# Cross-attention of a decoder layer: VectorE's instructions in written order, with the softmax cut into parts

## The chip, the cores and the metric

The kernel runs on one core of one Trainium2 chip. The metric is the device time in microseconds (us) of one execution; the number used for comparing is the median of several. A core has five engines that run side by side and wait for each other by semaphores: TensorE (PE in the profile, with its weight loads as PEld), VectorE (DVE), ScalarE (ACT), GpSimd (POOL) and SyncE (SP), which here issues most of the DMAs.

## The reference

One decoder layer on 32 sequences of 64 tokens (2048 rows) of width 512, all float32. Self-attention, cross-attention and a feed-forward block follow each other, each with a residual and a layer norm. The change touches only the cross-attention:

```python
q = (query @ Wq + bq).reshape(B, L, NKV, G, HDIM)      # 8 groups of G = 4 heads of 128
k_, v_ = jnp.split(kv @ Wkv + bkv, 2, axis=-1)
scores = jnp.einsum('blkgd,bmkd->bkglm', q, k) * scale # 64 x 64 for each sequence and head
attn = jax.nn.softmax(scores, axis=-1)
o = jnp.einsum('bkglm,bmkd->blkgd', attn, v).reshape(B, L, NHEAD * HDIM)
return o @ Wo + bo
```

Then `x = layernorm(x + that)`.

## The kernel before

**Stages.** Self-attention comes first, then the keys and values of the cross-attention (`keys_values`), then the cross-attention itself with the feed-forward block woven into its end. In the trace the cross-attention's first product starts at 2054.78 us.

**Units.** The cross-attention runs over 32 units, g (group of four heads, outer) by tb (block of 512 tokens, inner); N is 32. Iteration n of the main loop computes the queries and scores of unit n, and the attention output and output projection of unit n-1. So each iteration holds two big products: the queries of unit n (tiles `qx`, L282) and the projection of unit n-1 (tiles `wx`, L282).

**Seven products for eight.** Each big product is made of seven half-size products (Strassen's scheme in Winograd's form), called steps 1 to 7. A step is four matmuls in the code and eight in the trace, and fills one of three PSUM banks, x, y or z: steps 1 and 2 use x, steps 6, 7 and 4 use y, steps 5 and 3 use z. A later step of a bank adds onto what is in it, so it may start only when VectorE has read the bank as it stood before. For the projection these reads are additions into `acc` (L345, and L353 for the second read of step 1). The code's order of the steps is 1, scores, 6, 5, 2, 7, 3, 4 for the projection, and 1, 6, 5, 7, 2, 4, attention output, 3 for the queries. The next use of a bank thus sets a due time for a read: the read of step 7 (bank y) is due at step 4, with step 3 alone between them on PE; the read of step 6 is due at step 7, that of step 5 at step 3, that of step 1 at step 2. For the queries the read of step 6 (L322) is due at step 7, with step 5 between.

**The softmax of a unit** comes in two halves by tokens, pr = 0 and 1. For each: the largest score (L1056, VectorE), the difference (L1058, VectorE), the exponential (L1059, ScalarE), the sum (L1061), its reciprocal (L1062), the product with it (L1063) and a transpose in 32 x 32 blocks into tile T (L1068), the last four on VectorE. Then `move` issues eight DMAs from SP that put T into pT (L1082), which the next iteration's attention output (`attend`, PE L1103) reads.

**Who sets the order.** The loop runs under a manual schedule for PE and POOL: these two keep the order as written. VectorE, ScalarE and SP are ordered by a scheduler with its own costs, which moves their instructions among each other where dependencies allow. So VectorE's order in the program is not the code's: the scheduler puts the read of step 2 and the read of step 7 behind most of the softmax.

**The layer norm of a block** runs after the last group's projection of it (g = 7, iterations 29 to 32). `layernorm` at L1136 issues statistics (L149, L150), a sum (L151), a square root (ACT, L152), a reciprocal (L155) and four scalings (L157); the block's transposes (PE L129) are put off into the next iteration behind step 2 of its queries.

**POOL** makes sums of tokens (L1206 to L1211, `next_tokens`), of attention outputs (L256 to L259), of weights (L190 to L199) and, for g = 0, adds a bias to `acc` (L1261); all read and write SBUF.

Of the kernel before, what the change touches and what calls it, by code (L numbers as in the profile page):

```python
# [21 lines left out]
SEQ = 64  # L22
TB = 512
NTB = NT // TB
# [7 lines left out]
SQ = 32  # L32
# [20 lines left out]
def decoder_layer(  # L53
# [30 lines left out]
    nc = tc.nc  # L84
# [3 lines left out]
    small = ctx.enter_context(tc.tile_pool(name="small", bufs=4))  # L88
# [48 lines left out]
    def layernorm(tb, name):  # L137
        for part in layernorm_parts(tb, name):
            part()
# [324 lines left out]
    with ExitStack() as ph:  # L464
# [4 lines left out]
        sb = ph.enter_context(tc.tile_pool(name="sa", bufs=2))  # L469
# [168 lines left out]
        def turn(n, i):  # L638


            nc.vector.transpose(  # L641
                Ts[n][:, :, i, :], ps_.pop((n, i)).rearrange("q (b k) -> q b k", k=SQ)
            )

        def move(n, ranges=range(NQD), queue=nc.sync):


            if n // 2 not in pTs:
                pTs[n // 2] = sb.tile([P, NQD, NPC, P], F32, tag="pT", name=f"pT{n // 2}")
# [46 lines left out]
        N = len(units)  # L696
# [121 lines left out]
        for n in range(N):  # L818
            b, h = divmod(n, REP)
            g, r = units[n][0], n % PER  # L820
# [117 lines left out]
    with ExitStack() as ph:  # L938
# [14 lines left out]
        def load_xq(g):  # L953
            src = xwq[:, g * REP * HD : (g + 1) * REP * HD]
            wq_cur[g] = load_left(src, f"xwq{g}", nc.gpsimd)
# [91 lines left out]
                            )  # L1047
                ss[n, pr] = s

        def softmax(n, pr):  # L1050
            g, tb = units[n]
            u = f"x{g}_{tb}_{pr}"
            s = ss.pop((n, pr))
            shape = [P, 2 * REP, SEQ]
            mx = small.tile([P, 2 * REP], F32, tag="mx", name=f"mx{u}")
            nc.vector.tensor_reduce(mx, s, AX.X, ALU.max)  # L1056
            e = sb.tile(shape, F32, tag="e", name=f"e{u}")
            nc.vector.tensor_tensor(e, s, mx[:, :, None].to_broadcast(shape), ALU.subtract)  # L1058
            nc.scalar.activation(e, e, AF.Exp, scale=SCALE)  # L1059
            den = small.tile([P, 2 * REP], F32, tag="xden", name=f"den{u}")  # L1060
            nc.vector.tensor_reduce(den, e, AX.X, ALU.add)  # L1061
            nc.vector.reciprocal(den, den)  # L1062
            nc.vector.tensor_tensor(e, e, den[:, :, None].to_broadcast(shape), ALU.mult)  # L1063


            if pr == 0:
                Ts[n] = sb.tile([P, 2, TPB * REP, SQ], F32, tag="T", name=f"Tx{g}_{tb}", bufs=1)
            nc.vector.transpose(  # L1068
                Ts[n][:, :, pr * 2 * REP : (pr + 1) * 2 * REP, :].rearrange("p k r j -> p r k j"),
                e.rearrange("p r (k i) -> p r k i", i=SQ),  # L1070
            )

        def move(n):
# [54 lines left out]
        def project(n, *steps):  # L1128
            g, tb = units[n]
            for i in steps:  # L1130
                pjs[n].step(i)
                pjs[n].read()
            if steps[-1] == 4:
                del pjs[n]
                if g == NKV - 1:
                    layernorm(tb, "x")  # L1136
                    later.append(lambda: transpose_block(tb, "x2"))


# [74 lines left out]
        N = len(units)  # L1214
        load_kv(0)

        ph.enter_context(tc.manual_schedule(
            engines={mybir.EngineType.PE, mybir.EngineType.Pool}
        ))


        for n in range(N + 1):
            if n < N:
                g, tb = units[n]
                q = queries(n)
                for i in (1, 6, 5, 7):
                    q.step(i)
                    q.read()
                q.corner()
                q.step(2)  # L1230


                behind = g > 0 and tb == 1
                if not behind:
                    next_tokens(n + 1, 0)
            while later:
                later.pop(0)()
            if n < N:
                q.step(4)
                q.read()  # L1240
            if n > 0:
                attend(n - 1)
            if n < N:
                q.step(3)
                q.read()
                if behind:
                    next_tokens(n + 1, 0)
                next_tokens(n + 1, 1)
            if n == N:
                feed_forward(1)  # L1250
            if n > 0:
                project(n - 1, 1)
            if n < N:
                if n + 1 < N:
                    load_kv(n + 1)
                scores(n)
                softmax(n, 0)
            if n < N and g == 0:
                for j in range(TPB):
                    a = acc[tb][:, j, :]  # L1260
                    nc.gpsimd.tensor_tensor(a, a, bo, ALU.add)  # L1261
            if n > 0:
                project(n - 1, 6, 5)
            if n < N:
                softmax(n, 1)
                move(n)
                if tb == NTB - 1 and g + 1 < NKV:
                    load_xq(g + 1)
            if n > 0:
                project(n - 1, 2, 7, 3, 4)  # L1270
                if n < N and tb == 0:
                    if g > 0:
                        load_xo(g)
                    if g == NKV - 1:
                        load_ffn()
            if n == N - 1:
                feed_forward(0)
        feed_forward(2)
        while later:
            later.pop(0)()  # L1280
# [50 lines left out]
```

## Time and profile before

| what | us |
|---|---|
| median of 3 runs | 3100.44 (3098.5 to 3103.58) |
| the profiled execution: its own time | 3099.28 |
| the profiled execution: span from first to last instruction | 3097.0 |
| PE busy over the span | 3038.2 (98%) |
| VectorE busy | 2184.0 (71%) |
| POOL busy | 967.6 (31%) |
| ScalarE busy | 754.8 (24%) |
| self-attention, keys and values (0 to 2054.78) | 2054.78 |
| iterations 0 to 28 of the cross-attention, to the attention output of iteration 29 (2054.78 to 2894.10) | 839.32 |
| the last group's iterations with layer norms (2894.10 to 2977.80) | 83.70 |
| the feed-forward end (2977.80 to 3097.0) | 119.20 |

The granted TensorE clock is 0.998 over the span. In the stage from 2054.78 to 2894.10 PE is busy for 827.80 us of 839.32, VectorE for 515.24. Busy shares are averages: a matmul's end is modelled, and what an iteration could save is read from the places where PE stands still, and from the length of an iteration that has no such place. In the profile "issue" means that an engine waited for nothing that is shown, and "idle <- X" names what released it.

### The profile page before, as it was taken

The numbers are of one execution on the slowest core, as the hardware profiler recorded it, in microseconds if no ns is written. First come the engines' busy times: TensorE is split into PE (matmuls) and PEld (weight loads), VectorE is DVE, ScalarE is ACT, GpSimd is POOL, SyncE is SP. The second block draws the span as 40 slices with busy tenths as digits, with TensorE's granted clock in tenths as the row PEclk, the third lists the DMA queues.
The fourth block names the chain that finished last, engine by engine and source line by source line (L and its number), as shares of the span: only waits on it lengthen the run. The fifth ranks groups of instructions, "written<-read, shape, count | busy, mean of one in ns | idle before, by whom it ended". The sixth has DMA issues, their size and how long they took to land.

```text
span 3097.0 us, 42303 instructions
## 1 busy us (share of the span) xinstructions
PE 3038.2 (98%) x14944; PEld 2318.1 (75%) x14944; DVE 2184.0 (71%) x3957; ACT 754.8 (24%) x1760; POOL 967.6 (31%) x789
## 2 busy tenths in 40 slices
PE   8999999999999999999999999999999999999998
PEld 6777677777777777777677769988888888888864
DVE  6777777877877877877877754346656656656777
ACT  2323222222222232232322321211111111111132
POOL 4231321321322322323222122135444444444421
PEclk9999999999999999999999999999999999999999
DMA  6444444444444444444344343321121121121101
GB/s 206 116 114 119 113 115 123 111 122 114 108 128 112 106 128 113 107 125 118 101 123 109 98 126 128 109 103 48 50 67 48 51 66 48 51 66 48 49 28 41
DMA packets 200913, 298.66 MB, mean 96 GB/s; under 512 B 44160, under 2 KB 94848, under 8 KB 200704
## 3 DMA queue, kind: packets, MB, share of 16 engines
q1 hardware_dynamic: 187328, 282.51, 33.7%
q10 hardware_dynamic: 11328, 9.26, 1.0%
q0 software_dynamic: 2048, 4.20, 0.5%
q8 instruction: 120, 1.97, 0.3%
q14 instruction: 89, 0.73, 0.1%
HBM read 107.05 MB, written 20.97 MB: 41 GB/s over the span
## 4 chain that ended last, share of the span: by engine, by line
PE 86%; DVE 10%; DMA 1%; SPq 1%; issue 1%; ACT 1%; DVEq 0%; ACTq 0%
PE po L661 15%; PE s L615 15%; PE pox L1103 2%; DVE acc L345 2%; SPq L653 1%; PE w_0y L282 1%; PE q_3y L282 1%; PE w_3y L282 1%; PE qx_3y L282 1%; PE qx_2y L282 1%; PE qx_0y L282 1%; PE q_2y L282 1%; PE w_1y L282 1%; PE qx_1y L282 1%; PE wx_3y L282 1%; PE q_0y L282 1%
## 5 line engine op out<-in xcount | busy, mean ns | idle before, releaser
L623 ACT ACTIVATE p<-s,nmax 128x576 f32<-128x576 f32 x512 | 379.2, 741 | 1211.6 <-DVE nmax L620 1173.1
L615 PE MATMUL s<-kT,qT 128*128 128x288 f32 x2048 | 578.0, 408 | 11.5 <-ACT p L623 10.7
L661 PE MATMUL po<-pT,v 128*128 128x512 f32 (+1 forms) x1280 | 549.1, 602 | 4.3 <-DMA pT<-T 4.3
L615 PEld LDWEIGHTS s<-kT,qT 128*128 128x128 f32 x2048 | 387.4, 190 | 116.4 <-issue 20.1
L620 DVE TENSOR_REDUCE nmax<-s 128x1 f32<-128x576 f32 x512 | 384.0, 750 | 47.5 <-PE s L615 45.3
L641 DVE STREAM_TRANSPOSE T<-p 128x576 f32<-128x576 f32 x512 | 394.0, 769 | 4.4
L661 PEld LDWEIGHTS po<-pT,v 128*128 128x128 f32 (+1 forms) x1280 | 213.7, 189 | 204.2 <-issue 176.9
L633 DVE TENSOR_SCALAR p<-p,den 128x576 f32<-128x576 f32 x512 | 325.5, 636 | 17.9
L632 DVE RECIPROCAL den<-den 128x1 f32<-128x1 f32 x512 | 83.9, 164 | 238.2 <-ACT p L623 220.0
L256 POOL TENSOR_TENSOR so<-oT,oT 128x512 f32<-128x512 f32 x32 | 42.6, 1330 | 651.0 <-ACT oT L684 651.0
L258 POOL TENSOR_TENSOR so<-oT 128x512 f32<-128x512 f32 x32 | 40.7, 1272 | 334.4 <-PE w_1y L282 93.0
L1209 POOL TENSOR_TENSOR txx<-x1T 128x512 f32<-128x512 f32 x31 | 39.3, 1267 | 244.4 <-PE qx_3z L282 94.1
L197 POOL TENSOR_TENSOR tx<-xT 128x512 f32<-128x512 f32 x31 | 39.7, 1280 | 206.9 <-PE q_3z L282 65.5
L623 ACT ACTIVATION_READ_ACCUMULATOR p<-s,nmax 128x1 f32 x512 | 99.0, 193 | 0.0
L1059 ACT ACTIVATE ex<-ex 128x512 f32<-128x512 f32 x64 | 39.3, 630 | 203.1 <-DVE ex L1058 203.1
L256 POOL TENSOR_TENSOR sox<-oTx,oTx 128x512 f32<-128x512 f32 x32 | 40.5, 1266 | 149.7 <-DVE oTx L1123 144.3
L684 ACT COPY oT<-po 128x512 f32<-128x512 f32 x128 | 71.8, 586 | 44.9 <-PE po L661 44.1
L1043 PEld LDWEIGHTS sx<-kvx,qTx 128*64 128x64 f32 x2048 | 62.3, 138 | 10.6 <-issue 10.6
L1121 ACT ACTIVATE oTx<-pox,bv 128x256 f32<-128x256 f32 x128 | 52.0, 470 | 66.4 <-PE pox L1103 66.4
L1043 PE MATMUL sx<-kvx,qTx 128*64 128x64 f32 x2048 | 66.7, 224 | 0.0
L1103 PE MATMUL pox<-pTx,kvx 64*128 64x256 f32 x512 | 64.5, 389 | 0.1
L1123 DVE TENSOR_SCALAR oTx<-pox,bv 128x256 f32<-128x256 f32 x128 | 53.6, 478 | 9.8 <-PE pox L1103 9.8
(445 smaller groups left out, 5779.9 us busy)
## 6 DMA issues: line engine op xcount, KB each, us to landing
pT<-T SPq DMA_DIRECT2D x1020, 80.0 KB
pT<-T SPq DMA_DIRECT2D x1016, 64.0 KB
xT<-in_xT SPq DMA_DIRECT2D x31, 1024.0 KB
kvx<-kv SPq DMA_DIRECT2D x32, 512.0 KB
pTx<-Tx SPq DMA_DIRECT2D x256, 64.0 KB
kv<-c SPq DMA_DIRECT2D x30, 512.0 KB
wo<-in_woT SPq DMA_DIRECT2D x32, 256.0 KB
xwq<-in_xwq SPq DMA_DIRECT2D x32, 256.0 KB
```

The lines of the kernel that those rows point to most:

```text
L256: nc.gpsimd.tensor_tensor(t[1], a[1, 0], a[1, 1], ALU.add)
L282: nc.tensor.matmul(self.banks[b][:, m, :], self.left[i][:, k, m * P : (m + 1) * P], self.right[i][:, k, :], start=(first and m + k == 0), ...
L615: nc.tensor.matmul(s[:, a, :HALF], qTs[n // REP][:, units[n][2], i * P : (i + 1) * P], kTs[g][:, a * HALF : (a + 1) * HALF], start=True, s ...
L620: nc.vector.tensor_reduce(nmax, s[:, :, :HALF], AX.XY, ALU.max, negate=True)
L623: nc.scalar.activation(p.rearrange("q (a k) -> q a k", a=2), s[:, :, :HALF], AF.Exp, bias=nmax, accum_out=den,)
L632: nc.vector.reciprocal(den, den)
L633: nc.vector.tensor_scalar(p, p, den, None, ALU.mult)
L641: nc.vector.transpose(Ts[n][:, :, i, :], ps_.pop((n, i)).rearrange("q (b k) -> q b k", k=SQ))
L661: nc.tensor.matmul(pos[n].rearrange("d (a q) -> d a q", a=NQD), vs[units[n][0]][rows, v, :], pTs[n // 2][rows, :, chunk, :], skip_group_ch ...
L684: nc.scalar.copy(o[:, i, :].rearrange("d (t a k) -> d a t k", t=TPB, a=NQD), pos.pop(n - 1 + i).rearrange("d (a t k) -> d a t k", a=NQD, t ...
L1043: nc.tensor.matmul(s[b * SEQ : (b + 1) * SEQ, i * REP + h, :], qTs[n][:, h, pr * HF + c0 : pr * HF + c0 + SEQ], kvs[n][:, pr, 0, c0 : c0 + ...
L1103: nc.tensor.matmul(po[pr, b][:, i, :].rearrange("d (h a j) -> d h a j", h=REP, a=2), kvs[n][r, pr, 1, i * HD : (i + 1) * HD], pTs[n][r, :, ...
```

## The change

VectorE joins the engines under the manual schedule for iterations 0 to 30; at iteration 31 that schedule is closed and one for PE and POOL alone is opened, as before. `softmax` is cut into five parts (`largest`, `exponentials`, `denominators`, `weights`, `turn`), and these are called for both halves between the steps of the projection, in this order: step 1, scores; largest 0 and 1; exponentials 0 and 1; step 6; denominators 0 and 1; step 5; weights 0; steps 2 and 7; weights 1; step 3; turn 0 and 1; `move`; step 4. A `Projection` step's read is issued right after its product. `load_xq` of the next group is written ahead of steps 2 and 7. The layer norm of a block is split: statistics and square root directly after step 4, the reciprocal and scalings from a list `scales`, which is emptied after the first query step of the next iteration that has one, and ahead of the transposes.

In the built program the order of instructions on PE, ScalarE and POOL stays as it was. On SP, in the seven iterations that load the next group's output weights, the fourth of these loads (`xwo_3`) now stands ahead of the eight DMAs of `move` and not behind them. On VectorE the instructions are the same in number and kind, in another order.

```diff
-        def softmax(n, pr):
+        def largest(n, pr):
+            mxs[pr] = small.tile([P, 2 * REP], F32, tag="mx", name=f"mx{n}_{pr}")
+            nc.vector.tensor_reduce(mxs[pr], ss[n, pr], AX.X, ALU.max)
+        def exponentials(n, pr):
...
+            nc.vector.tensor_tensor(e, s, mxs[pr][:, :, None].to_broadcast(shape), ALU.subtract)
             nc.scalar.activation(e, e, AF.Exp, scale=SCALE)
+        def denominators(n, pr):
+            nc.vector.tensor_reduce(den, es[pr], AX.X, ALU.add)
+        def weights(n, pr):
             nc.vector.reciprocal(den, den)
+            nc.vector.tensor_tensor(
+                e, e, den[:, :, None].to_broadcast([P, 2 * REP, SEQ]), ALU.mult
+            )
+        def turn(n, pr):
...
             nc.vector.transpose(
...
-                    layernorm(tb, "x")
+                    stats, scale = layernorm_parts(tb, "x")
+                    stats()
+                    scales.append(scale)
                     later.append(lambda: transpose_block(tb, "x2"))
...
-        ph.enter_context(tc.manual_schedule(
-            engines={mybir.EngineType.PE, mybir.EngineType.Pool}
-        ))
+        units_order.enter_context(tc.manual_schedule(engines={
+            mybir.EngineType.PE, mybir.EngineType.Pool, mybir.EngineType.DVE
+        }))
...
         for n in range(N + 1):
+            if n == N - 1:
+                units_order.close()
+                ph.enter_context(tc.manual_schedule(
+                    engines={mybir.EngineType.PE, mybir.EngineType.Pool}
+                ))
...
                 for i in (1, 6, 5, 7):
                     q.step(i)
                     q.read()
+                    while scales:
+                        scales.pop(0)()
...
                 scores(n)
-                softmax(n, 0)
+            parts(n, (largest, 0), (largest, 1), (exponentials, 0), (exponentials, 1))
...
+            steps(n - 1, 6)
+            parts(n, (denominators, 0), (denominators, 1))
+            steps(n - 1, 5)
+            parts(n, (weights, 0))
+            if n < N and tb == NTB - 1 and g + 1 < NKV:
+                load_xq(g + 1)
+            steps(n - 1, 2, 7)
+            parts(n, (weights, 1))
+            steps(n - 1, 3)
+            parts(n, (turn, 0), (turn, 1))
+            if n < N:
+                move(n)
             if n > 0:
-                project(n - 1, 6, 5)
-            if n < N:
-                softmax(n, 1)
-                move(n)
-                if tb == NTB - 1 and g + 1 < NKV:
-                    load_xq(g + 1)
-            if n > 0:
-                project(n - 1, 2, 7, 3, 4)
+                steps(n - 1, 4)
```

More of the change, by code (lines that the diff above doesn't have):

```diff
@@ L1048, in scores @@
                 ss[n, pr] = s
-        def softmax(n, pr):
+        def largest(n, pr):
+            mxs[pr] = small.tile([P, 2 * REP], F32, tag="mx", name=f"mx{n}_{pr}")
+            nc.vector.tensor_reduce(mxs[pr], ss[n, pr], AX.X, ALU.max)
+        def exponentials(n, pr):
             g, tb = units[n]
-            u = f"x{g}_{tb}_{pr}"
             s = ss.pop((n, pr))
             shape = [P, 2 * REP, SEQ]
[L1055 to L1058, printed above, removed]
+            es[pr] = e = sb.tile(shape, F32, tag="e", name=f"ex{g}_{tb}_{pr}")
+            nc.vector.tensor_tensor(e, s, mxs[pr][:, :, None].to_broadcast(shape), ALU.subtract)
             nc.scalar.activation(e, e, AF.Exp, scale=SCALE)
-            den = small.tile([P, 2 * REP], F32, tag="xden", name=f"den{u}")
-            nc.vector.tensor_reduce(den, e, AX.X, ALU.add)
-            nc.vector.reciprocal(den, den)
-            nc.vector.tensor_tensor(e, e, den[:, :, None].to_broadcast(shape), ALU.mult)
+        def denominators(n, pr):
+            dens[pr] = den = small.tile([P, 2 * REP], F32, tag="xden", name=f"denx{n}_{pr}")
+            nc.vector.tensor_reduce(den, es[pr], AX.X, ALU.add)
+        def weights(n, pr):
+            e, den = es[pr], dens[pr]
+            nc.vector.reciprocal(den, den)
+            nc.vector.tensor_tensor(
+                e, e, den[:, :, None].to_broadcast([P, 2 * REP, SEQ]), ALU.mult
+            )
+        def turn(n, pr):
+            g, tb = units[n]
             if pr == 0:
@@ L1069, in softmax @@
                 Ts[n][:, :, pr * 2 * REP : (pr + 1) * 2 * REP, :].rearrange("p k r j -> p r k j"),
-                e.rearrange("p r (k i) -> p r k i", i=SQ),
+                es[pr].rearrange("p r (k i) -> p r k i", i=SQ),
             )
@@ L1215, in decoder_layer, with parts, steps @@
         load_kv(0)
-        ph.enter_context(tc.manual_schedule(
-            engines={mybir.EngineType.PE, mybir.EngineType.Pool}
-        ))
-        for n in range(N + 1):
+        units_order = ExitStack()
+        units_order.enter_context(tc.manual_schedule(engines={
+            mybir.EngineType.PE, mybir.EngineType.Pool, mybir.EngineType.DVE
+        }))
+        def parts(n, *made):
+            for part, pr in made:
+                if n < N:
+                    part(n, pr)
+        def steps(n, *made):
+            if n >= 0:
+                project(n, *made)
+        mxs, es, dens, scales = {}, {}, {}, []
+        for n in range(N + 1):
+            if n == N - 1:
[3 more added lines that the diff above has]
+                ))
             if n < N:
@@ L1235, in decoder_layer @@
                     next_tokens(n + 1, 0)
+            while scales:
+                scales.pop(0)()
             while later:
@@ L1250, in decoder_layer @@
                 feed_forward(1)
-            if n > 0:
-                project(n - 1, 1)
+            steps(n - 1, 1)
             if n < N:
@@ L1261, in decoder_layer @@
                     nc.gpsimd.tensor_tensor(a, a, bo, ALU.add)
-            if n > 0:
-                project(n - 1, 6, 5)
-            if n < N:
-                softmax(n, 1)
-                move(n)
-                if tb == NTB - 1 and g + 1 < NKV:
-                    load_xq(g + 1)
-            if n > 0:
-                project(n - 1, 2, 7, 3, 4)
+            steps(n - 1, 6)
[8 more added lines that the diff above has]
+            parts(n, (turn, 0), (turn, 1))
+            if n < N:
+                move(n)
+            if n > 0:
+                steps(n - 1, 4)
                 if n < N and tb == 0:
@@ L1277, in decoder_layer @@
                 feed_forward(0)
+        scales.pop(0)()
         feed_forward(2)
```

## The prediction, made before the changed kernel ran

> **What bounds the kernel now.** I read the busy table first (PE 98%), then what PE waits for in the cross-attention, from the first attention output to the feed-forward (2081 to 2978 us). Columns: us in total, times, longest.
>
> ```profile
> PE wx_2y L282 <- DVE acc L345: 6.8, 8, 0.9
> PE wx_0y L282 <- DVE acc L345: 3.8, 8, 0.6
> PE wx_1y L282 <- DVE acc L345: 1.3, 2, 0.7
> PE x L129 <- ACT qTx L317: 1.0, 2, 0.5
> PE x L129 <- DVE x1T L131: 0.6, 2, 0.3
> ```
>
> PE stands still 18 times for a projection read on VectorE, 11.9 us in all. The weight load runs ahead of the matmuls and has to be refilled after a stop, so the loss is larger. The table of stages, cut at the starts of two successive attention outputs (L1103), gives it (columns: stage, length, busy time of PE, PEld, DVE, ACT, POOL, clock, DMA share, GB/s):
>
> ```profile
> 2256.18:2285.87 29.69, 28.77 (x194) 24.44 (x194) 18.64 (x32) 4.27 (x9) 15.37 (x12) 1.00 0.18 49
> 2285.87:2314.38 28.51, 28.51 (x194) 24.52 (x194) 17.43 (x32) 4.27 (x9) 9.86 (x8) 1.00 0.28 75
> ```
>
> The second has no stop and takes 28.51, all of it PE; the first has one stop of 0.92 and is 1.18 longer. So a stop costs 0.26 to 0.27 beyond its idle time, and 28.51 is PE's floor for an iteration. The 28 stretches from 2081.20 to 2894.10 take 812.90; at the floor 28 x 28.51 = 798.28. Excess 14.6. Why VectorE is late shows in the timeline of a stalled iteration (start, length, idle before):
>
> ```profile
> 2384.11 1.26 POOL L192 TENSOR_TENSOR xwq<-xwq,xwq 128x512 f32<-128x512 f32 x1
> 2384.31 1.61 DVE L1063 TENSOR_TENSOR ex<-ex,denx 128x512 f32<-128x512 f32 x1
> ...
> 2387.53 0.68 DVE L345 TENSOR_TENSOR acc<-wx_2x,acc 128x512 f32<-128x512 f32 x1
> 2388.13 0.70 DVE L1068 STREAM_TRANSPOSE Tx<-ex 128x512 f32<-128x512 f32 x1
> 2388.75 0.65 DVE L345 TENSOR_TENSOR acc<-wx_2y,acc 128x512 f32<-128x512 f32 x1
> 2388.85 4.95 SPq L1082 DMA_DIRECT2D pTx<-Tx  x8
> 2389.33 0.67 DVE L345 TENSOR_TENSOR acc<-wx_2z,acc 128x512 f32<-128x512 f32 x1
> 2389.45 1.59 PEld L282 LDWEIGHTS wx_2y<-xwo,oTx 128*128 128x128 f32 x8 [1.32 <-DVE acc L345]
> 2389.45 1.99 PE L282 MATMUL wx_2y<-xwo,oTx 128*128 128x256 f32 x8 [0.92 <-DVE acc L345]
> ```
>
> The read of step 7 stands behind both products and both transposes of the softmax. A product (L1063) that meets a POOL instruction takes 1.61 instead of 0.65; its median over all 64 is 0.68, its longest 1.63. That tips the scheduler's order over: step 7's read comes at 2388.75, after PE has finished step 3. Iterations in which POOL is quiet have the same order and no stop.
>
> **Part 1: the new order, step by step.** I count from the start of step 6 on PE (2379.64 in the iteration shown), with 1.73 for a product and 0.60 from one VectorE instruction to the next. A read can start 0.20 after its product's nominal end. Unchanged up to the differences: step 6's read at 2.22. Sums 2.8 to 4.0. Step 5's read 4.0 to 4.6. Reciprocal, then product 0 from 4.8 to 5.4 (6.3 if blocked as shown). Step 2's read is ready at 5.4, so done by 6.0 (6.9 if blocked). Step 7's read is ready at 7.1 and done at 7.75, while PE wants it at 8.6, after step 3. Margin 0.85 in quiet and busy iterations. Product 1 from 7.9 to 8.5, step 3's read 8.8 to 9.4, the transposes to 10.7, step 4's read to 11.3. The other due times: step 6's read 2.8 against 5.2, step 5's 4.6 against 6.9, and step 4's 11.3 against 13.8 (its bank comes round to the third query product). So the 18 stops go. What is late next on PE? Nothing but itself, in these stretches.
>
> Of the 14.6 above, 0.37 of the first stretch are no stop (its first attention output took 2.28, not 1.93): 14.2. Iterations 29, 30 and 31 lie behind 2894.10 and have a stop each, idle 0.46, 0.61 and 0.61, so about 0.7, 0.9 and 0.9: 2.5. Iteration 31 is ordered by the scheduler again; in the built program step 7's read there stands behind one product and one transpose only, which fits. Gain of part 1: 16.7.
>
> **The rule weighed.** Product 0 still stands ahead of step 7's read. [...] Blocked by two (2 x 1.27), product 0 ends at 8.0 and step 7's read at 9.2: 0.6 late, 0.9 with the refill, in the same 18 iterations, and part 1 gains nothing. The row speaks for one: none of 64 exceeded 1.63. I take the row.
>
> **Part 2: what else moves.** `move`: the transposes end at 10.7 instead of 9.2 (7.9 when quiet), so its eight DMAs start 1.5 to 2.9 later; issuing them takes 4.95. The attention output that needs them starts at 21.0. In iteration 0 the first was issued at 2075.09 and the attention output ran at 2081.13 without waiting, so they land in 6.0 or less: by 16.9. Cover 4.1; without it each us costs 31 us over the kernel. SP: `xwo_3` now goes ahead of them in seven iterations; it waits for step 3, done at 8.6, and one such issue takes 0.37, so it is gone before 10.8. It lands earlier than before, which only helps POOL's sums (L196). `load_xq` keeps its place on SP. New semaphore waits: VectorE now waits for PE at each read with product 1, the transposes and so on queued behind; all these have the margins above. Zero.
>
> **Part 3: iteration 0.** Nothing is projected, so the new order only changes the halves' interleaving: product 0 now waits for its reciprocal directly (about 0.2), and difference 0 waits behind largest 1, whose scores end at 2069.05. I get the transposes' end 0.35 later. There PE already waited 1.3 for the query read behind them (qx_1y for L322). Loss 0.35 (bounds 0 and 0.8).
>
> **Part 4: iteration 30, the layer norm.** Statistics and scalings of block 0 are now ordered by the code, ahead of the read of the query's step 6 (L322), which step 7 of the queries needs. Before:
>
> ```profile
> 2915.28 0.17 DVE L151 TENSOR_SCALAR rstd_x<-mv_x 128x4 f32<-128x4 f32 x1
> ...
> 2916.53 0.69 DVE L322 TENSOR_TENSOR qTx<-qx_2y,qTx 128x512 f32<-128x512 f32 x1 [1.08 <-PE qx_2y L282]
> 2916.63 0.21 ACT L152 ACTIVATE rstd_x<-rstd_x 128x4 f32<-128x4 f32 x1
> 2917.14 0.17 DVE L155 RECIPROCAL rstd_x<-rstd_x 128x4 f32<-128x4 f32 x1
> 2917.35 3.85 DVE L157 TENSOR_SCALAR acc<-acc,mv_x,rstd_x 128x512 f32<-128x512 f32 x4
> 2917.78 1.70 PEld L282 LDWEIGHTS qx_2y<-txx,xwq 128*128 128x128 f32 x8
> 2917.99 1.89 PE L282 MATMUL qx_2y<-txx,xwq 128*128 128x256 f32 x8
> ```
>
> The read slipped in ahead of the scalings. Now count from the first query product: step 4's read ends at 1.0; four blocks' statistics at 0.84 each (0.72 to the aggregate, 0.12 more) bring L151 to 4.4; the square root to 4.8 (its table load fits behind the first query copy); reciprocal 5.1; scalings from 5.3. Alone four of them take 1.92 (as at 2949.77), against POOL's token sums 3.85 as here: to 7.25 or 9.15. These sums are there again, from 5.4. L322 ends at 7.9 or 9.8; PE wanted it at 5.2. Loss 2.7 or 4.6 idle, 3.0 or 4.9 with the refill. I take 4.8, since two of POOL's three sums fall there (the third waits for step 7 itself). Iteration 31's query read is put ahead by the scheduler again (done at 4.8 against 5.2), and the transposes follow as before: zero, at most 1.
>
> **Sum.** 16.7 - 0.35 - 4.8 = 11.5. The profiled execution took 3099.28 (span 3097.0 and 2.3 around it): 3087.8. The median of the runs is 1.16 higher: 3100.44 - 11.5 = 3088.9.
>
> **Rivals.**
> - *Iteration 30 costs less*: scalings that miss POOL, or start earlier: 1 to 3. Gain 13.5 to 16: 3084.5 to 3087. For it: the bound 3.0. Against: POOL's sums are released by PE at the same moment. 0.10.
> - *Half of the stops stay or move*: product 0 or 1 meets POOL twice, or a read in written order misses its slot in some iterations. Gain 2 to 9: 3091.5 to 3098.5, about 3095. Against: margin 0.85 and the longest row 1.63. 0.13.
> - *The DMAs of `move` come late* (slower): they decide once the time from first issue to landing passes 10.2. At 11.2, 31 attention outputs wait 1.0: 31 - 11.5, so 3120. For it: `move` is the one thing that got later in every iteration. Against: 6.0 seen, DMA share 0.14 to 0.28 there. 0.03.
> - *It doesn't do what it says*: VectorE's order unchanged in effect. The built program's order on VectorE is the written one, so I give it nothing beyond the second rival.
>
> **How the numbers follow.** The forecast (gain 9 to 14) has 0.74. A measurement here can tell about 0.2%, 6.2 us, from no change. Faster by more: 0.74 + 0.10 and a little under half of the second rival, 0.05: 0.89. Same: 0.08. Slower: 0.03. The range reaches from 3084 (iteration 30 nearly free) to 3095 (the middle of the second rival).
>
> **What would show it.** Right: the rows "wx_y waits for acc L345" are gone; all stretches between attention outputs of iterations 2 to 28 are 28.5; step 7's read starts 0.2 after its product; PE waits some 4.6 once, for L322, near iteration 30; `move` starts about 2 later with no wait of L1103 for it. Wrong: L1063 rows above 2 us, PE stops at the end of iterations, waits of L1103 for pTx, or a stop at iteration 31.

## The result, and the profile after

| | median, us | runs | ratio to the kernel before, 95% interval |
|---|---|---|---|
| kernel before | 3100.16 (3098.5 to 3103.58) | 6 | |
| kernel after | 3088.3 (3087.27 to 3089.18) | 6 | 0.9962 (0.9951 to 0.9973) |

The change saves 11.9 us, or 0.38%. The predicted time was 3088.9. The profiled execution after took 3088.83 with a span of 3085.9, against 3099.28 and 3097.0 before: 11.1 less in the span. In the kernel after, the lines of the softmax are L1052 (largest), L1059 (difference), L1064 (sum), L1068 (reciprocal), L1069 (product), L1079 (transpose) and L1093 (`move`); the attention output is L1114, and POOL's sums of tokens are L1219 to L1224. The lines ahead of the softmax keep their numbers (L282, L322 and L345 among them).

First what PE waits for from the first attention output to the feed-forward, in the kernel after (us in total, times, longest; the two rows of `x L129` follow, as long as before):

```profile
PE qx_2y L282 <- DVE qTx L322: 4.1, 1, 4.1
PE pox L1114 <- DMA pTx<-Tx: 1.1, 1, 1.1
```

The 18 waits of a projection product for `acc` (11.9 us in all) are gone. Two new rows stand in their place, each with one wait: 4.1 for the query read in iteration 30, and 1.1 for the moved softmax in iteration 1. The table of stages of the kernel after (stage, length, busy time of PE, PEld, DVE, ACT, POOL, clock, DMA share, GB/s) holds the 28 stretches of the prediction in one row, from the end of the wait for pTx on, and the stretch that ends with iteration 30's attention output in the next:

```profile
2081.35:2879.68 798.33, 798.33 (x5376) 686.83 (x5376) 504.09 (x894) 119.97 (x252) 365.39 (x289) 1.00 0.20 56
2879.68:2918.32 38.64, 33.78 (x211) 28.06 (x210) 26.81 (x48) 6.83 (x13) 14.11 (x11) 0.91 0.10 28
```

In the first PE is busy for the whole length, and 798.33 / 28 = 28.51: the floor, in every iteration. In the second it stands still for 38.64 - 33.78 = 4.86, and the mean granted clock is 0.91. The timeline of the iteration that the prediction showed with a stop, now (start, length, idle before):

```profile
2378.49 1.26 POOL L192 TENSOR_TENSOR xwq<-xwq,xwq 128x512 f32<-128x512 f32 x1
2378.84 1.46 DVE L1069 TENSOR_TENSOR ex<-ex,denx 128x512 f32<-128x512 f32 x1
...
2381.23 0.69 DVE L345 TENSOR_TENSOR acc<-wx_2y,acc 128x512 f32<-128x512 f32 x1 [0.33 <-PE wx_2y L282]
...
2382.75 1.89 PE L282 MATMUL wx_2y<-xwo,oTx 128*128 128x256 f32 x8
...
2383.56 1.29 DVE L1079 STREAM_TRANSPOSE Tx<-ex 128x512 f32<-128x512 f32 x2
...
2384.88 4.95 SPq L1093 DMA_DIRECT2D pTx<-Tx  x8
```

The first product, with a POOL sum 0.35 ahead of it, still runs long (1.46; the median of all 64 is 0.69). But step 7's read no longer stands behind the second product and the transposes: VectorE even waits 0.33 for step 7 to end on PE, reads at 2381.23, and step 4 starts on PE at 2382.75 without an idle time. `move` starts 10.87 after the start of step 6 (2374.01); the prediction had 10.8.

Where the 11.1 of the span went, by the same cuts in both traces, after minus before: start of the kernel to cross-attention's first product -1.82; from there to the query product behind the first attention output +1.65; the 28 stretches -14.25; the next (iteration 30) +6.38, which is -0.7 for the stop before it and +7.1; the next two -0.87 and -0.88; last `pu` product -1.66; the rest +0.36. The first of these and that of the last `pu` lie outside the change; they come back at the end.

### The profile page after: what moved, and what is told of

Its sections match the earlier page's. It is cut to its first block, busy times and chain, and to the rows that moved or that the text cites. A ratio compares the mean times of both kernels' runs of the same rounds, so it can differ in the third digit from the quotient of the medians.

```text
span 3085.9 us, 42306 instructions
## 1 busy us (share of the span) xinstructions
PE 3034.2 (98%) x14944; PEld 2320.6 (75%) x14944; DVE 2186.5 (71%) x3957; ACT 757.2 (25%) x1760; POOL 967.6 (31%) x789
## 3 DMA queue, kind: packets, MB, share of 16 engines
q8 instruction: 120, 1.97, 0.3%
## 4 chain that ended last, share of the span: by engine, by line
PE 91%; DVE 4%; DMA 2%; SPq 2%; ACT 1%; issue 1%; ACTq 0%; DVEq 0%
PE po L661 15%; PE s L615 15%; PE sx L1043 2%; PE pox L1114 2%; PE w_0y L282 1%; PE q_3y L282 1%; PE wx_2y L282 1%; PE wx_1y L282 1%; PE w_3y L282 1%; SPq L653 1%; PE qx_2y L282 1%; PE qx_3y L282 1%; PE qx_0y L282 1%; PE w_1y L282 1%; PE q_2y L282 1%; PE wx_0y L282 1%
## 5 line engine op out<-in xcount | busy, mean ns | idle before, releaser
L1114 PE MATMUL pox<-pTx,kvx 64*128 64x256 f32 x512 | 64.9, 390 | 1.1 <-DMA pTx<-Tx 1.1
```

Of the source, the lines that this page charges most:

```text
L1114: nc.tensor.matmul(po[pr, b][:, i, :].rearrange("d (h a j) -> d h a j", h=REP, a=2), kvs[n][r, pr, 1, i * HD : (i + 1) * HD], pTs[n][r, :, ...
```

## The experiments

Theory A is the prediction's: half of the softmax stood ahead of step 7's read, POOL tipped that into 18 stops, and the new order removes them at the price of one wait in iteration 30. After the result it has one addition: that wait costs more than its idle time, because the clock falls behind it (0.91 in that stretch, where the other 28 have 1.00). The rivals are named at each experiment. The kernel before was run again beside each group of experiments: its median was 3098.11 beside the first four, 3099.44 beside the next four and 3098.30 beside the last four. "The stretch of iteration 30" below is the one from the attention output before it to its own: 38.64 in the kernel after, 32.26 in the kernel before, which is 31.54 without the stop in it (0.46 and 0.26 to refill). The refill is what a stop cost beyond its idle time, 29.69 - 28.51 - 0.92 = 0.26 in the prediction's stages; at the stop in its timeline PEld stood still for 1.32 and PE for 0.92.

**1. Scalings behind the read** (`e1_scale_after_read`, and once more beside the changed kernel below).

```diff
-                    while scales:
+                    while scales and i == 6:
                         scales.pop(0)()
```

> The changed kernel, with one difference: in iteration 30 the reciprocal and the four scalings of the layer norm stand behind the read of the query's step 6, and not ahead of it. Theory A (the pause of 4.05 us there costs its length and also makes TensorE run at half clock for some 3 us afterwards, 7.1 in all): the stretch between the attention outputs of iterations 29 and 30 goes from 38.64 to about 31.6, clock 1.00 in it, and the time goes to 3088.3 - 7.1 = 3081.2. Theory B (only the pause and the refill count, 4.3, as in the prediction's sum; the slow matmuls come from elsewhere): 3084.0, with slow matmuls still in that stretch. Both: nothing else changes.

3084.63 in five runs (3079.94 to 3085.33), ratio 0.9956 (0.9943 to 0.997). The median is near B's 3084.0; what tells the theories apart is the stretch. No wait for L322, no slow product; the stretch is 32.39 with the clock at 1.00, where B had slow products still. What it has above 31.54 is a wait of the transposes that is 1.16 and not 0.31 long, since the scalings now hold up the eviction of the block's first transposes. So the loss in iteration 30 comes from this one read standing behind the scalings.

**2. Iteration 0 as before** (`e2_first_unit_as_before`).

```diff
-            nc.vector.reciprocal(den, den)
+            if n > 0:
+                nc.vector.reciprocal(den, den)
+            elif pr == 0:
+                for d in (dens[0], dens[1]):
+                    nc.vector.reciprocal(d, d)
...
-            parts(n, (largest, 0), (largest, 1), (exponentials, 0), (exponentials, 1))
+            if n == 0:
+                parts(n, (largest, 0), (exponentials, 0), (largest, 1), (exponentials, 1))
+            else:
+                parts(n, (largest, 0), (largest, 1), (exponentials, 0), (exponentials, 1))
```

> The changed kernel, with iteration 0 alone in the order that the scheduler gave it before (largest 0, difference 0, largest 1, difference 1; both reciprocals ahead of both products). From the first query product to the third query step of iteration 1 behind the attention output, the trace showed 28.63 us before and 30.28 after. Theory A (the new order in iteration 0 makes the eight DMAs of the move start later, and the attention output waits for them): back to about 28.6, no wait for pTx. Theory B (the order costs 0.3 only; the 1.1 of waiting for pTx came with the issuing of the DMAs, 6.32 us instead of 4.95, which varies on its own): the wait for pTx is there or not whatever the order, and the stretch is 28.6 to 30.0 with the pause of 1.56 for the query read down to 1.3. Time about 3087 to 3088.

One run, 3088.6, no faster than the changed kernel: here the last `pu` was slow (5.33), which comes back at the end. From the first query product to `qx_1z` behind the first attention output it takes 28.63, as before; the kernel after took 30.28. Both waits are back to what they were: 1.29 ahead of `qx_1y`, none for pTx. By that alone the order would cost the 1.65; experiments 10 to 12 showed that this reading was wrong.

**3. The order written out, without the cut** (`e3_written_order_uncut`): the kernel before with VectorE under the manual schedule as well.

```diff
-        ph.enter_context(tc.manual_schedule(
-            engines={mybir.EngineType.PE, mybir.EngineType.Pool}
-        ))
+        units_order = ExitStack()
+        units_order.enter_context(tc.manual_schedule(engines={
+            mybir.EngineType.PE, mybir.EngineType.Pool, mybir.EngineType.DVE
+        }))
...
+            if n == N - 1:
+                units_order.close()
+                ph.enter_context(tc.manual_schedule(
+                    engines={mybir.EngineType.PE, mybir.EngineType.Pool}
+                ))
```

> The kernel before, with VectorE under the manual schedule in iterations 0 to 30 but the softmax not cut: half 0 whole, then the reads of steps 6 and 5, then half 1 whole, then the other reads; the layer norm as before. Theory A (what counts is when the read of step 7 is done against the end of step 3): counted from step 6's start, half 0 holds VectorE to 4.6, step 6's read ends at 5.2, half 1 ends at 10.5, step 2's read at 11.1, step 7's at 11.7 against 8.6. A pause of some 3 us and the refill in each of 30 iterations: 3100 + 30 x 3.3 = about 3200 as long as the clock holds, and up to 3290 if pauses of that length halve the clock for some 3 us each. Theory B (the manual order as such makes the gain, the cuts are decoration): about 3088.

One run, 3183.39: 85 us slower than before. What PE waits for from the first attention output to 3000 us, and one of these stops in the timeline:

```profile
PE wx_0y L282 <- DVE acc L345: 19.9, 9, 2.4
PE wx_2y L282 <- DVE acc L345: 16.8, 8, 2.4
PE wx_1y L282 <- DVE acc L345: 16.7, 8, 2.4
...
```

```profile
2266.78 0.71 DVE L1068 STREAM_TRANSPOSE Tx<-ex 128x512 f32<-128x512 f32 x1
2267.42 0.65 DVE L345 TENSOR_TENSOR acc<-wx_1x,acc 128x512 f32<-128x512 f32 x1
2268.00 0.68 DVE L345 TENSOR_TENSOR acc<-wx_1y,acc 128x512 f32<-128x512 f32 x1
2268.59 0.67 DVE L345 TENSOR_TENSOR acc<-wx_1z,acc 128x512 f32<-128x512 f32 x1
...
2268.73 1.99 PE L282 MATMUL wx_1y<-xwo,oTx 128*128 128x256 f32 x8 [2.25 <-DVE acc L345]
```

With each half of the softmax in one piece, three reads come in a row when the second half is through, and PE stops for 2.25 to 2.4 in nearly every iteration; stretches are 31.0 and more. The mechanism is A's, its price smaller than the 3.1 that I had reckoned. Without the cut, the softmax by halves in written order loses.

**4. The kernel before, without POOL's bias sums** (`e4_before_no_bias`). The four sums with the output bias in the first group are left out, so the output lacks that bias.

```diff
-            if n < N and g == 0:
-                for j in range(TPB):
-                    a = acc[tb][:, j, :]
-                    nc.gpsimd.tensor_tensor(a, a, bo, ALU.add)
```

> The kernel before without the additions of the output bias to the accumulators on POOL in the first four iterations, so its output lacks that bias. The order on VectorE is the same as in the kernel before. Theory A (a stop comes about only where a product of the softmax meets a POOL instruction): the first group's stops at wx_0y, wx_1y and wx_2y vanish, these three stretches go from 29.5 to 28.5 each, and the other stops stay; in the first group the products L1063 take 0.65 to 0.7. Time about 3097.5. Theory B (the scheduler's order is late by itself, POOL only happens to be busy): the three stops stay at 0.6 to 0.9, time 3100.

One run, 3095.14, 3.0 below its kernel before. What PE waits for from 2045 us to the end (before: 6.8 in 8, 3.8 in 8, 1.3 in 2):

```profile
PE wx_2y L282 <- DVE acc L345: 6.2, 7, 0.9
PE wx_0y L282 <- DVE acc L345: 3.1, 7, 0.4
...
PE wx_1y L282 <- DVE acc L345: 0.6, 1, 0.6
```

VectorE's instructions and their order are those of before; only POOL is quieter in the first group. One stop of each row is gone. In the first group the stops of iterations 1 and 2 went (the stretch of iteration 2 fell from 29.48 to 28.51; that of iteration 1 is as long as before, since a wait of 0.6 for pTx came in). The third, of iteration 3, which A had expected to go too, stays (29.71): there POOL also sums weights, and the first product took 1.63. The other stop that went is that of iteration 27, where POOL's work is as before. The timeline there:

```profile
2847.04 0.68 DVE L1063 TENSOR_TENSOR ex<-ex,denx 128x512 f32<-128x512 f32 x1
2847.14 1.71 POOL L192 TENSOR_TENSOR xwq<-xwq,xwq 128x512 f32<-128x512 f32 x1
```

This time the product starts 0.10 ahead of POOL's sum and takes 0.68, and the sum takes 1.71. In the kernel before the sum started first (2847.90, 1.26 long, against 2848.09), the product took 1.62, and PE stopped for 0.92; now step 7's read is done in time, and the stretch is 28.76 for 29.71. So with the same instructions in the same order the stop was there where POOL's sum had started first (by 0.19), and gone where the product had (by 0.10): two traces of one place. I read from them that it is POOL beside an order with too little room that makes the stops.

**5 to 7. The changed kernel again, experiment 1 again, and both edits together, on one chip.**

> The changed kernel as it is, beside the next two kernels on one chip. It should come 11 to 12 us below the kernel before, as it did (3088.3 against 3100.2). Theory A (iteration 30's pause before qx_2y is the term that I priced too low, 7.1 us instead of 4.8): here again a pause of about 4 us before qx_2y with the granted clock near 0.5 in the microseconds behind it, and a stretch to that attention output of 38 to 39 us. Theory B (the slow clock behind that pause was chance in one profile): the pause is there and the clock stays near 1, stretch near 36.4.

> Reciprocal and scalings of the layer norm put behind step 6's read instead of ahead of it in iteration 30, all else as in the changed kernel. Theory A: the pause before qx_2y goes, and with it about 6.2 us (stretch 32.4 instead of 38.6), so 6 us below the changed kernel on the same chip. Theory B: 36.4 - 32.4 = 4 us below it. If it comes within 2 us of it, the time that the pause costs is given back somewhere behind, and the place has to be looked for.

> As the last, and the first group's softmax in the order of before in iteration 0 (the parts by half only from iteration 1 on). Theory A (the order in iteration 0 costs the 0.3 us that the prediction gave it, and the 1.65 us of the first profile was mostly the eight DMAs' longer issue, which comes and goes): 0.3 us below the last kernel, not to be told from it by the medians. Theory B (the order brings the whole 1.65): 1.3 to 1.7 us below it.

| kernel | median of 5, us | ratio to before | stretch of iteration 30 |
|---|---|---|---|
| changed kernel | 3088.51 (3086.64 to 3089.77) | 0.9964 (0.9951 to 0.9978) | 37.51, clock 0.95 |
| scalings behind the read | 3084.33 (3082.83 to 3087.64) | 0.9952 (0.9938 to 0.9965) | 32.38, clock 1.00 |
| both edits | 3083.77 (3081.16 to 3084.82) | 0.9947 (0.9933 to 0.9961) | 34.06, clock 0.95 |

The pause before `qx_2y` is 4.05 again in the changed kernel, and the clock falls again, this time for a shorter while: 37.51 against 38.64. Moving the scalings takes 5.1 from the stretch, and 4.2 from the median; that lies between what A (6) and B (4) had. So the fall of the clock is no chance of one profile, but its length differs. The kernel with both edits is the best of these three, by less than the runs scatter, which decides nothing between its A and B; its stretch shows a slow product behind two short waits (0.49 and 1.15), which I come back to.

**8. Three more maxima ahead of step 7's read** (`e5_three_more`).

```diff
-            steps(n - 1, 2, 7)
+            steps(n - 1, 2)
+            if 0 < n < N - 1:
+                for _ in range(3):
+                    pad = small.tile([P, 2 * REP], F32, tag="pad", name=f"pad{n}_{_}")
+                    nc.vector.tensor_reduce(pad, es[1], AX.X, ALU.max)
+            steps(n - 1, 7)
```

> The changed kernel with three more maxima of 128x512 -> 128x2 on VectorE ahead of step 7's read in each iteration between the first and the last (their results are used by nothing). It tests the margin of 0.85 us that the prediction gave step 7's read. Theory A (the margin is real and small): three maxima are about 1.8 us, against 0.33 us of idle time and 0.85 of margin in the 18 or so iterations in which VectorE is slowed by GpSimd, so PE waits some 0.6 us there, and 0.27 to refill: 18 x 0.9 = 16 us above the changed kernel, and pauses of 0.3 to 1 us before the product behind step 7's read. Theory B (the read is not what ends next, the slack in VectorE's row is larger): within 2 us of the changed kernel and no new pauses.

3098.71 in 12 runs, 10.2 above the changed kernel on the same chip. What its projection waits for up to iteration 29, and one of these stops in the timeline:

```profile
PE wx_2y L282 <- DVE acc L345: 2.7, 7, 0.4
PE wx_0y L282 <- DVE acc L345: 1.8, 6, 0.3
...
PE wx_1y L282 <- DVE acc L345: 0.2, 1, 0.2
```

```profile
2267.58 1.48 DVE L1069 TENSOR_TENSOR ex<-ex,denx 128x512 f32<-128x512 f32 x1
...
2269.59 1.85 DVE L1308 TENSOR_REDUCE pad<-ex 128x8 f32<-128x512 f32 x3
...
2271.36 0.67 DVE L345 TENSOR_TENSOR acc<-wx_2y,acc 128x512 f32<-128x512 f32 x1
...
2272.09 1.99 PE L282 MATMUL wx_2y<-xwo,oTx 128*128 128x256 f32 x8 [0.44 <-DVE acc L345]
```

The three maxima delay the next start by 2271.36 - 2269.59 = 1.77, and PE now stops for 0.44. Of the 1.77, 0.33 was idle time, so the read had 1.77 - 0.33 - 0.44 = 1.0 of room in a busy iteration: 0.85 was predicted. Stops come in these 14 iterations, those in which POOL is busy, and their stretches are together 8.5 longer than the floor, 0.6 each, and not 18 times 0.9. B, that the read is not what ends next, falls.

**9. The cut alone** (`e7_cut_scheduler`): the changed kernel with VectorE left to the scheduler.

```diff
-            mybir.EngineType.PE, mybir.EngineType.Pool, mybir.EngineType.DVE
+            mybir.EngineType.PE, mybir.EngineType.Pool
```

> The changed kernel with VectorE's order in cross-attention left to the scheduler as before: only the cut of the softmax into parts by half stays. In the built order step 7's read stands behind one product and one transpose instead of two and two, and the layer norm's scalings of iteration 30 stand ahead of the query's read. Theory A (the cut brings most of the gain, by taking one product and one transpose, 1.3 to 2.2 us, from in front of step 7's read): of the 18 stops, 0.9 us on average, none or a few small ones of up to 0.6 stay; stretches 28.5 to 29.1, and about 3088 (3084 to 3092). Theory B (the order written by hand is what brings the gain, and the scheduler's order loses it again): stops of 0.6 to 1.3 as before in half of the iterations, and within 3 us of the kernel before.

3084.97 in five runs (3083.93 to 3087.82), ratio 0.9959 (0.9946 to 0.9973): at the lower end of what A had, and far from B. A busy iteration in its timeline:

```profile
2265.00 1.46 DVE L1069 TENSOR_TENSOR ex<-ex,denx 128x512 f32<-128x512 f32 x1
...
2266.98 1.15 DVE L1069 TENSOR_TENSOR ex<-ex,denx 128x512 f32<-128x512 f32 x1
...
2268.06 0.70 DVE L1079 STREAM_TRANSPOSE Tx<-ex 128x512 f32<-128x512 f32 x1
2268.69 0.65 DVE L345 TENSOR_TENSOR acc<-wx_2y,acc 128x512 f32<-128x512 f32 x1
...
2269.39 1.99 PE L282 MATMUL wx_2y<-xwo,oTx 128*128 128x256 f32 x8 [0.32 <-DVE acc L345]
```

Step 7's read stands behind both products (the expectation had one), both slowed by POOL, and one transpose, and is 0.32 late. Six stops of this length and two of 0.09 stay up to iteration 29, and the 28 stretches are 4.6 above the floor together; behind them there is none. In iteration 30 the scheduler puts the query's read ahead of the scalings, as it did in the kernel before (the expectation had it behind them), and the stretch is 31.54 without a pause for it. So in the 28 stretches the cut alone takes 9.7 of the 14.25, the written order the other 4.6, and in iteration 30 the written order gives back 5.8 to 7.1 (stretches of 37.31 to 38.64).

**10. Two scalings ahead of the read and two behind it** (`e6_two_scalings`).

```diff
-        def scale():
-            nc.vector.reciprocal(rstd, rstd)
-            for j in range(TPB):
+        def scale(j0=0, j1=TPB):
+            if j0 == 0:
+                nc.vector.reciprocal(rstd, rstd)
+            for j in range(j0, j1):
...
-                    scales.append(scale)
+                    scales.extend((lambda: scale(0, 2), lambda: scale(2, 4)))
...
-                    while scales:
-                        scales.pop(0)()
+                    if i in (1, 6):
+                        while scales and (i == 1) == (len(scales) == 2):
+                            scales.pop(0)()
```

> The changed kernel with two of the layer norm's four scalings put ahead of step 6's read in iteration 30 and two behind it. Theory A (the size of the loss comes from two things: the pause itself, and a granted clock near 0.5 behind it once the pause is long enough): the pause before qx_2y falls from 4.05 to 2.0 to 2.3, the clock stays near 1.0 behind it, the stretch is 31.6 + 2.5 = 34 us instead of 38.6, and the time about 4.5 below the changed kernel's. Theory B (the slow clock follows any pause of some 2 us): the products behind it take 2.5 to 3.8 us again, the stretch 35.5 to 37.

3083.83 in five runs (3080.61 to 3086.84), ratio 0.9954 (0.994 to 0.9967). In its own lines, which stand one further down, the timeline and a table of stages of iteration 30 (columns as above):

```profile
2903.18 1.00 DVE L158 TENSOR_SCALAR acc<-acc,mv_x,rstd_x 128x512 f32<-128x512 f32 x2
...
2904.09 0.68 DVE L323 TENSOR_TENSOR qTx<-qx_2y,qTx 128x512 f32<-128x512 f32 x1
2904.69 2.30 DVE L158 TENSOR_SCALAR acc<-acc,mv_x,rstd_x 128x512 f32<-128x512 f32 x2
2904.92 1.97 PE L283 MATMUL qx_2y<-txx,xwq 128*128 128x256 f32 x8 [1.24 <-DVE qTx L323]
...
2906.72 1.89 PE L283 MATMUL qx_2x<-x1T,xwq 128*128 128x256 f32 x8
```

```profile
2880.28:2913.30 33.02, 30.98 (x209) 26.10 (x209) 26.13 (x48) 6.82 (x13) 14.10 (x11) 1.00 0.12 33
```

The first two scalings are not slowed by POOL (1.00 for both; its first sum starts at 2903.77, while the second scaling runs, and takes 1.53), so the pause is 1.24, shorter than the 2.0 to 2.3 expected; the products behind it run at full clock, and the stretch costs 33.02 - 31.54 = 1.48, that is 1.24 and 0.24 to refill. That is what A has for a short pause. B, which was about pauses of some 2 us, is not tested by one of 1.24. This kernel surprised me elsewhere: its order in iteration 0 is that of the changed kernel, and still it shows no wait for pTx. From the first query product to `qx_1z` it takes 28.89, 0.26 above the kernel before.

**11 and 12. Which half of the reordering in iteration 0** (`e10_first_exponentials`, `e11_first_reciprocals`): each keeps one of the two edits of experiment 2.

> The changed kernel; only in iteration 0 each half's differences follow its maxima directly again (maximum 0, differences 0, maximum 1, differences 1), while the reciprocals stay by half. From the first query product to qx_1z behind the first attention output the kernel before took 28.63, the changed one 29.7 to 30.3 in four profiles. Theory A (waiting for the second half's scores ahead of the first half's differences starts the exponentials late): 28.8 or less, the pause before qx_1y about 1.3 and no wait for pTx. Theory B (it is the reciprocals by half): 29.7 or more, as in the changed kernel.

> The counterpart of the last: in iteration 0 both reciprocals stand together ahead of both products again, while the maxima of both halves stay ahead of the differences. Theory A: 29.6 or more from the first query product to qx_1z, with a wait for pTx of 0.5 or more. Theory B: 28.8 or less and no such wait. If both of these kernels show 29.7, either one alone is enough to delay the landing; if both show 28.6, it takes the two together.

One run each: 3087.92 and 3088.71. The first takes 30.02 from the first query product to `qx_1z` and pauses 1.52 ahead of `qx_1y`; the second 29.99 and 1.31. They wait 0.84 and 1.03 for pTx. So the reciprocals by half bring the 0.2 to 0.3 ahead of `qx_1y`; the wait for pTx follows neither edit. What it goes with was found in the DMA view. The queues in the first 7 us from the first DMA of `move` on, in the changed kernel (packets, MB, share of 16 engines):

```profile
q1 hardware_dynamic: 342, 0.47, 30.0%
q8 instruction: 1, 0.02, 1.4%
```

and the same 7 us of the kernel with two scalings ahead of the read:

```profile
q1 hardware_dynamic: 384, 0.52, 32.9%
```

In the second all 384 packets are through; the instruction packet comes later, alone, and takes 1.1 us of one DMA engine. In nine of the 14 profiles (the changed kernel twice, experiments 1 and 6, 4, 8, 9, 11 and 12) this one packet comes 4.4 to 5.1 us behind the issue of the first DMA, amid the packets of `move`, takes 0.9 to 1.5 us of an engine, and PE waits 0.5 to 1.1 for pTx. In the other five (the kernel before, experiments 2, 3, 7 and 10) it comes at 7.4, and PE does not wait for pTx. In experiment 2 the packet thus lay elsewhere too, and my reading there, which put the whole 1.65 down to the order, left that out.

## Why the prediction was right, and which terms were off

**Part 1, the stops: right in mechanism and size.** Predicted 14.2 in the 28 stretches and 0.7, 0.9, 0.9 behind them; measured 14.25, 0.7, 0.87 and 0.88. The floor of 28.51 holds in every stretch. Experiment 4 shows POOL as the tipping cause, experiment 8 the room of 1.0 for 0.85, and experiment 3 that the written order needs the cut.

**Two POOL instructions ahead of product 0: the row was right.** I had set a product 0 held up by two of them (2 x 1.27) against the longest product of before, 1.63. In the kernel after the longest of all 64 products is 1.47, shorter than two POOL instructions, and there is no such stop.

**Part 2, `move` and the queues: zero, right.** `move` starts 1.66 later than before (10.87 for 9.21 behind step 6) in the iteration shown, and only one attention output waits for it: that of iteration 1, for the `move` of iteration 0, in which nothing is projected, and for another reason (part 3).

**Part 3, iteration 0: 0.35 predicted, 1.65 in this trace.** The order itself costs 0.26 (experiment 10, where it stands alone). The rest is the wait for pTx, 1.06, and what goes with it. It coincides with one instruction packet of 0.02 MB amid those of the eight DMAs. The kernel before without POOL's bias sums has it too (0.6, packet at 4.8), with VectorE's old order. That the packet delays them is an inference from where it lies in 14 profiles; no kernel here moves it and nothing else, so the cause of this wait stays open. My bound of 0.8 did not hold because the sum had no term for a late landing in iteration 0.

**Part 4, iteration 30: the term that was mis-sized.** The step said: L322 ends at 9.8 behind the first query product, PE wanted it at 5.2, 4.6 idle and with the refill 4.8 to 4.9. The timeline of the kernel after:

```profile
2902.51 3.81 DVE L157 TENSOR_SCALAR acc<-acc,mv_x,rstd_x 128x512 f32<-128x512 f32 x4
2903.10 1.54 POOL L1222 TENSOR_TENSOR txx<-x1T 128x512 f32<-128x512 f32 x1 [10.26 <-PE qx_2z L282]
2904.71 1.33 POOL L1223 TENSOR_TENSOR txx<-x1T,txx 128x512 f32<-128x512 f32 x1
2906.24 0.68 DVE L322 TENSOR_TENSOR qTx<-qx_2y,qTx 128x512 f32<-128x512 f32 x1
2907.07 3.75 PE L282 MATMUL qx_2y<-txx,xwq 128*128 128x256 f32 x8 [4.05 <-DVE qTx L322]
2910.61 2.96 PE L282 MATMUL qx_2x<-x1T,xwq 128*128 128x256 f32 x8
```

The scalings meet POOL's two sums, 3.81 as predicted (3.85). They start at 4.84 behind the first query product (2897.67) instead of 5.3, so the idle time is 4.05 (the square root's table load, 1.28 from 2900.20, was over before the sum that the root waits for). But then the two products take 3.75 and 2.96 where 1.89 is usual. Stages of 3.41 us around the pause (clock third from the right):

```profile
2902.52:2905.93 3.41, 0.50 (x3) 0.09 (x1) 3.41 (x4) 0.00 (x0) 2.75 (x2) 1.00 0.22 51
2905.93:2909.35 3.42, 2.28 (x6) 1.86 (x7) 0.99 (x2) 0.00 (x0) 0.11 (x1) 0.50 0.00 0
2909.35:2912.76 3.41, 3.41 (x10) 2.69 (x9) 1.57 (x3) 0.00 (x0) 1.27 (x1) 0.50 0.00 0
2912.76:2916.17 3.41, 2.61 (x18) 1.95 (x17) 0.69 (x1) 1.82 (x4) 0.00 (x0) 1.00 0.00 0
```

So the loss is 38.64 - 31.54 = 7.1: 4.05 idle and 3.05 for refill and slow clock. (Experiment 9, which has no stop and no such pause there, has the 31.54 as it is.) The failed term is a missing one: I priced a pause of 4.6 by its length and the refill, and put the clock behind it at nothing. The stages are cut where the clock changes: it is at half for two of them, 6.83 us. Of what PE does in them, 2.28 + 3.41, half is lost, 2.85; 38.64 - 31.54 - 4.05 - 0.26 leaves 2.79. In the repeated run of the changed kernel the pause is 4.05 too; the clock is 0.80, 0.50 and 0.82 in the stretches 2907.70 to 2909.70, to 2911.70 and to 2913.40, which comes to 3.41 us at half. By the same working that costs 1.7, and measured are 37.51 - 31.54 - 4.05 - 0.26 = 1.66.

**The sum.** With the measured terms of the change, this pair of traces gives -16.7 + 1.65 + 7.1 = -7.95. The other -3.1 lie outside it. At the start, `q_1z` stands behind a pause of 3.83 or 3.84 in all traces; it took 3.78 before and 2.52 after, with 6.83 us at half clock before (from 47.37) and 3.41 after (from 48.98). At the end, the last `pu` stands behind one of 1.84; it took 5.37 before, with 3.41 us at half clock (from 3064.76), and 3.67 after, at full clock, and both lengths turn up among the experiments (5.22 to 5.37 in six of them) without relation to their edits. So that the forecast of -11.5 was met this closely is in part luck: two costs were 1.3 and 2.3 too low, and 3.1 came from the clock in places that the change does not touch. How much of this is in the medians, which differ by 11.9 and 10.9 in the two comparisons, profiles of single executions can't say; it stays open.

**Rivals.** No stop stays or moves, an attention output waits for `move` once, in iteration 1 (such waits I had named as a sign of being wrong), and none does in the iterations that follow, and iteration 30 is dearer, not cheaper. What I had not thought of is the version with the cut alone, whose time is at least as good as that of the change as made.

## What to carry to other kernels

When an order is written by hand for a loop, it also fixes the few iterations that differ from the others; look for what the scheduler had got right there, and leave those to it or write them apart: here one misplaced block of four scalings gave back 6 to 7 of 17 us in the profiles. Price a long stall of the matmul engine with what the clock takes behind it, not by its idle time alone: behind the pause of 4.05 it took 2.8 us in one trace and 1.7 in another. And cut a vector stage where a bank's read has to come between, before writing any order: the cut alone brought most of the gain.

## What the runs showed of the hardware

The granted clock behind some pauses of PE (us; the clock as the stages show it):

| trace | behind | idle of PE | what followed |
|---|---|---|---|
| after | iteration 30, `qx_2y` | 4.05 | 0.50 for 6.83; the products took 3.75 and 2.96 |
| after, repeated | iteration 30, `qx_2y` | 4.05 | 0.50 for 3.41 |
| before | `q_1z` | 3.83 | 0.50 for 6.83; it took 3.78 |
| after | `q_1z` | 3.84 | 0.50 for 3.41; it took 2.52 |
| before | last `pu` | 1.08, 1.84 | 0.50 for 3.41; it took 5.37 |
| after | last `pu` | 1.07, 1.83 | 1.00; it took 3.67 |
| two scalings (10) | iteration 30, `qx_2y` | 1.24 | 1.00; the products took 1.97 and 1.89 |
| scalings behind the read (6) | iteration 30, transposes | 1.16 | 1.00 over the stretch |

So half clock followed the four longest pauses of the table, for 3.41 or 6.83 us, and at the last `pu` it followed two pauses in one trace and not in the other, where they were as long to 0.01. `q_1z` shows the same spread: behind 3.83 or 3.84 in all 14 traces, it took from 1.99 (experiment 3) to 3.78 (before, experiments 6 and 12). In the kernel with both edits the waits of 0.49 and 1.15 lie in the first of these two stages, and the second is at half clock:

```profile
2906.97:2910.38 3.41, 1.76 (x14) 1.24 (x13) 2.98 (x5) 1.80 (x4) 0.63 (x1) 1.00 0.00 0
2910.39:2913.80 3.41, 3.41 (x11) 2.64 (x9) 0.69 (x1) 0.00 (x0) 0.00 (x0) 0.50 0.02 5
```

What decides, beside the length of a pause, whether and for how long the clock falls is not shown here; it stays open.

One instruction packet of 0.02 MB took 0.9 to 1.5 us of a DMA engine, and PE waited for pTx in the nine profiles in which it lay amid the packets of `move`, not in the five in which it did not; one of these, experiment 3, had more room (9.0 us from the first issue to the attention output, for 6.0 in the kernel before). Issuing the eight DMAs of iteration 0 took 4.95 from SP in the kernel before and 6.32 in the kernel after, where one of the eight took 1.96, with a median of 0.59.
